# Convolution chain on one core: products of layer 0 ordered by row groups, waves of the tail joined into two double waves a step

## The chip, the core and the metric

The kernel runs on one core of one Trainium2 chip. The metric is the device time of one execution in microseconds (us). The kernel before takes 5648.19 us, the median of three runs (5645.71 to 5648.49). Differences below about 0.2%, some 11 us, can't be told from no change here.

## What is computed

The input x is 4 x 16 x 512 x 512 in f32 (batch, channels, rows, columns). Four layers follow each other. Cut to what matters:

```python
# layer 0: depthwise 3x3 convolution added to x, attention in 8x8 windows (2 heads of 8), MLP
x = x + depthwise3x3(x, pos_w) + pos_b
q, k, v = qkv(aff1(x))                      # per window of 64 positions
x = x + softmax(q @ k.T * 8**-0.5) @ v @ proj_w.T + proj_b
x = x + gelu(aff2(x) @ fc1_w.T + fc1_b) @ fc2_w.T + fc2_b
# layer 1: fake-quantised 3x3 convolution, batch norm over the whole output, clip to 0..6
z = clip(batch_norm(conv3x3(quant(x), quant(weight))), 0, 6)
# layer 2: two 3x3 convolutions with a residual
x = conv3x3(relu(conv3x3(z, w1) + b1), w2) + b2 + z
# layer 3: 3x3 convolution, then 16 -> 128 -> 16 pointwise, with a residual
out = x + w2 @ relu(w1 @ conv3x3(x) + b1) + b2
```

## The kernel before

**Three stretches.** The layer 0 stretch (`window_attention`, L144) lasts to about 3150 us; a statistics pass of layer 1 (L1026 to L1053) has its products from 3166 to 3449 us; and the tail, with its first product at 3461 us, runs layers 1 to 3 as one pipeline over 128 groups of rows (L1228 to L1242) to the end. In all of them the order of instructions on each engine is the order in which the code emits them (`manual_schedule`): every engine works its list in order and waits where an operand or a buffer isn't ready.

**Layer 0.** There are 64 steps. A step has 128 partitions (four row quarters of 32, called quads) and four column parts of 512 positions. The helper `quad(i)` picks partitions 32i to 32i+31. Most products are 32x32 weights against 512 positions: the input's quad selects a row group of the TensorE array, the output's quad a column group. Such an f32 product appears in the trace as two records of its line, so 16 products of all 16 tiles are 32 records.

A step first runs the score part (`values`, `scores`, `attend`, `divide`, `turn_back`, L519 to L541). Then come 16 blocks "qqddddqqqqdddddd" (L543): a "q" is a query product of the next step (L314, evicted by ACT at L319 here), a "d" is one tap of the depthwise convolution of the step after (L287), four products of one row group. The queries use PSUM banks 4, 5, 6, 7, 4, 5 in this order (L542). Then `project(y)` (L547, products at L404) multiplies the attention output `o` by the two heads' weights, 2 x 16 products, into the same banks 4 to 7: part u goes into bank 4 + (u + 2) % 4, that is 6, 7, 4, 5. DVE adds each bank to `y[:, u]` (L409, four instructions, u = 0 first). After that 44 blocks "ddddhdhddhqq..." (L558) run; an "h" is the hidden layer of the MLP for one part (L416, evicted by ACT with GELU at L421) and reads `y[:, u]`, the first three with u = 0.

Ahead of the loop, the depthwise convolution of steps 0 and 1 runs alone: nine taps of 16 products each (L489 to L492), row group u outside, column part vv inside.

**The tail.** Step T runs these on TensorE, in this order: `outputs(T-7)` (L1217, 16 products of 128x32 weights), `wave(T-6, 0)` (L1197, four products of 32x128 weights, one a row group), `stage_y(T-4)`, `wave(T-6, 1)`, `stage_x(T-3)`, `wave(T-6, 2)`, `stage_h(T-1)`, `stage_z(T)`, `wave(T-6, 3)`. The four stages are 3x3 convolutions of 24 products of 64x32 weights each (`convolve`, L1122; `stage_z` in bf16). PSUM banks are handed out in rotation by `take` (L961): 2 for a convolution, 4 for a wave, 2 for the outputs, of 8 in all. A convolution's first bank is evicted by ACT and its second by DVE (L1181/L1182 for `stage_y`, L1159/L1160 for `stage_h`, L1141/L1142 for `stage_z`); both banks of `stage_x` by DVE (L1170). The banks of a wave are evicted by DVE (L1207, first and third) and ACT (L1205, second and fourth). DVE also scales the next input (L1010), clips `ze` in place (L1143) and adds the outputs (L1223).

SP issues the DMAs of a step in the order of the code: the load of T+3 (L940, 2), the store of the outputs (L1226, 1), and four each for `qo` (after the rounding on ACT, L1013), `xo`, `ho` and `zo` (L1064 and L1067), which copy a stage's rows to the partitions where the next stage reads them.

Of the kernel before, what the change touches and what calls it, by code (L numbers as in the profile page):

```python
# [29 lines left out]
TP = H // 4  # L30
NH, HD = 2, 8
WS = 8
T = WS * WS
# [71 lines left out]
def conv_chain(ctx: ExitStack, tc: tile.TileContext, x, xw, mats, vecs, cqs, cws, hots, out):  # L105
# [29 lines left out]
    nc.gpsimd.memset(peak, 0.0)  # L135

    safe = window_attention(tc, xw, x1, hots, m, v, peak)
    with tc.If(safe == 0):
        attention_block(tc, x, x1, m, v, peak)
# [4 lines left out]
def window_attention(ctx: ExitStack, tc, xw, x1, hots, m, v, peak):  # L144
# [15 lines left out]
    U = V = 4  # L160
# [14 lines left out]
    def bank(i):  # L175
        return pairs[i // 2][:, i % 2, :] if i < 4 else singles[i - 4]

    def quad(i):
        return slice(32 * i, 32 * i + 32)
# [3 lines left out]
    def load(k):  # L183
        t = xin.tile([P, V, WS + 2, BW + 2], F32, tag="x", name=f"x{k}")
        nc.sync.dma_start(t, xw[k])
        return t
# [93 lines left out]
    def by_row(ap):  # L280
        return ap.rearrange("p (a j x) -> p a j x", a=WS, x=WS)

    def depthwise(n, tap, u):

        dy, dx = divmod(tap, 3)
        for vv in range(V):
            nc.tensor.matmul(  # L287
                bank(u)[quad(vv)], taps[quad(u), tap, :],
                xts[n][quad(u), vv, dy : dy + WS, dx : dx + BW],
                start=tap == 0, stop=tap == 8,  # L290
            )

    def position(n, i):

        if n not in ys:
            ys[n] = px.tile([P, U, N], F32, tag="y", name=f"y{n}", bufs=3)
        for u in (2 * i, 2 * i + 1):
            nc.vector.tensor_scalar(  # L298
                by_window(ys[n][:, u]), by_row(bank(u)), v("pos_b"), None, ALU.add
            )  # L300
# [98 lines left out]

    def project(y):  # L400
        for h in range(NH):
            for u in range(U):
                for vv in range(V):
                    nc.tensor.matmul(  # L404
                        bank(4 + (u + 2) % 4)[quad(vv)], wo[h][quad(u)], o[quad(u), vv, :, h, :],
                        start=h == 0, stop=h == 1,
                    )
        for u in range(U):
            nc.vector.scalar_tensor_tensor(  # L409
                y[:, u], bank(4 + (u + 2) % 4), pb, y[:, u], ALU.add, ALU.add  # L410
            )
# [76 lines left out]
    )  # L488
    for n in range(2):  # L489
        for tap in range(9):  # L490
            for u in range(U):
                depthwise(n, tap, u)  # L492
        xts[n + 2] = load(n + 2)
        for i in range(2):
            position(n, i)
# [8 lines left out]
    for n in range(STEPS):  # L504
# [40 lines left out]
        if more:  # L545
            highest(n + 1)
        y = ys.pop(n)  # L547
        project(y)
        if n % 2 == 0:
            xo = px.tile([P, U, WS, XW], F32, tag="xo", name=f"xo{n}", bufs=1)  # L550
# [5 lines left out]
        hids, units, sent = [[] for _ in range(U)], itertools.cycle((6, 7, 4, 5)), 0  # L556
        used = [0] * U
        for i, what in enumerate("ddddhdhddhqqhddhdhddhdhddhddhddhdhddddhhddhh"):  # L558
            if what == "h":
                at = i % 4  # L560
                u = used[at]
# [364 lines left out]
def _quad(i):  # L926
    return slice(32 * i, 32 * i + 32)
# [19 lines left out]
def conv_layers(ctx: ExitStack, tc, x1, out, cw, cq, sw, m, v, peak):  # L947
# [13 lines left out]
    def take(n):  # L961
        return [banks[next(turn) % 8] for _ in range(n)]
# [3 lines left out]
    def ring(name, n, dt=F32):  # L966
        tiles = rings[name] = [
            act.tile([P, 2, WP], dt, name=f"{name}{i}") for i in range(n)
        ]
        return lambda k: tiles[k % n]  # L970
# [6 lines left out]
    ze, zo, he, ho = ring("ze", 4), ring("zo", 3), ring("he", 2), ring("ho", 2)  # L977
# [19 lines left out]
    def inner(t):  # L997
        return t[:, :, 1 : W + 1]
# [3 lines left out]
    def load(n, dst=None):  # L1002
        if dst is None:
            dst = ld.tile([P, 2, W], F32, tag="x", name=f"tx{n}")
        loaded[n] = dst
        _load_pairs(nc, dst, x1, n)
# [62 lines left out]
    def quantised(n):  # L1069
        scaled(n)  # L1070
        rounded(n)
        shift(n, qe, qo, n < TP)
# [39 lines left out]
    def convolve(weights, pair):  # L1112

        p = take(2)
        for dx in range(3):
            for w in range(2):
                if pair[w] is None:
                    continue
                src, odd = pair[w]
                for f in range(2):  # L1120
                    for r in range(2):
                        nc.tensor.matmul(  # L1122
                            p[r][_quad(2 * f + w)], weights[_half(r), odd, dx, :],
                            src[_half(r), f, dx : dx + W],
                            start=dx == 0, stop=dx == 2,
                        )
        return p

    def shift_ends(n, e, o):

        shift(n, e, o, ends=True)
        if n == TP - 1:
            for i in (0, 2):
                nc.gpsimd.memset(o(n)[_quad(i)], 0.0)

    def stage_z(n):

        if not 0 <= n < TP:
            return
        p, z = convolve(cq, ((qe(n), 0), (qo(n), 1))), inner(ze(n))  # L1140
        nc.scalar.activation(z[:, 0], p[0], AF.Identity, bias=shift_by, scale=scale)  # L1141
        nc.vector.tensor_scalar(z[:, 1], p[1], scale, shift_by, ALU.mult, ALU.add)  # L1142
        nc.vector.tensor_scalar(z, z, ACT_MAX, 0.0, ALU.min, ALU.max)  # L1143
        shift_ends(n, ze, zo)

    def stage_h(n):

        if not 0 <= n <= TP:
            return
        second = (ze(n), 0) if n < TP else None  # L1150
        p, h = convolve(cw[:, 0], ((zo(n - 1), 1), second)), inner(he(n))
        if n in (0, TP):
            e = slice(n // TP, n // TP + 1)
            for f in range(2):
                nc.scalar.activation(
                    h[:, f], p[f], AF.Relu, bias=edge_b1[:, e], scale=v("edge")[:, e]
                )
        else:
            nc.scalar.activation(h[:, 0], p[0], AF.Relu, bias=v("l2_b1"))  # L1159
            nc.vector.tensor_scalar(h[:, 1], p[1], v("l2_b1"), 0.0, ALU.add, ALU.max)  # L1160
        shift(n, he, ho, n < TP)

    def stage_x(n):

        if not 0 <= n < TP:
            return
        p = convolve(cw[:, 1], ((he(n), 0), (ho(n), 1)))
        x, z = inner(xe(n)), inner(ze(n))
        for r in range(2):
            nc.vector.scalar_tensor_tensor(  # L1170
                x[:, r], p[r], v("l2_b2"), z[:, r], ALU.add, ALU.add
            )
        shift_ends(n, xe, xo)

    def stage_y(n):

        if not 0 <= n <= TP:
            return
        second = (xe(n), 0) if n < TP else None
        p, y = convolve(cw[:, 2], ((xo(n - 1), 1), second)), inner(ye(n))  # L1180
        nc.scalar.copy(y[:, 0], p[0])  # L1181
        nc.vector.tensor_copy(y[:, 1], p[1])  # L1182
# [5 lines left out]
    def wave(n, k):  # L1188

        if not 0 <= n < TP:  # L1190
            return []
        units, p = [], take(4)
        for q in range(4):
            w, f = divmod((k + q) % 4, 2)
            par = w ^ (q % 2)
            src = ye(n + (w and not q % 2))
            nc.tensor.matmul(  # L1197
                p[q], w1[_quad(q), 1 - par, :], inner(src)[_quad(q), f, :],
                start=True, stop=True,
            )  # L1200
        for q in range(4):
            w, f = divmod((k + q) % 4, 2)
            hd = ld.tile([P, W], F32, tag="hid", name=f"hid{n}_{k}_{q}", bufs=24)
            if next(count) % 2:
                nc.scalar.activation(hd, p[q], AF.Relu, bias=v("l3_b1"))  # L1205
            else:
                nc.vector.tensor_scalar(hd, p[q], v("l3_b1"), 0.0, ALU.add, ALU.max)  # L1207
            units.append((q // 2, 2 * f + w, w ^ (q % 2), hd))
        return units

    def outputs(n, units):

        if not units:
            return
        p, o, seen = take(2), inner(xe(n)), set()
        for r, c, par, hd in units:
            nc.tensor.matmul(  # L1217
                p[r][_quad(c)], w2[:, par], hd,
                start=(r, c) not in seen, stop=(r, c) in seen,
            )  # L1220
            seen.add((r, c))
        for r in range(2):
            nc.vector.scalar_tensor_tensor(  # L1223
                o[:, r], p[r], v("l3_b2"), o[:, r], ALU.add, ALU.add
            )
        nc.sync.dma_start(out[n], o)  # L1226

    units = []  # L1228
    for T in range(TP + 7):
        if T + 3 <= TP:  # L1230
            load(T + 3)
        outputs(T - 7, units)
        units = wave(T - 6, 0)
        stage_y(T - 4)
        units += wave(T - 6, 1)
        if T + 2 <= TP:
            quantised(T + 2)
        stage_x(T - 3)
        units += wave(T - 6, 2)
        stage_h(T - 1)  # L1240
        stage_z(T)
        units += wave(T - 6, 3)  # L1242


def _strips(a):
# [127 lines left out]
```

## Time and profile before

| What | us |
|---|---|
| median of three runs | 5648.19 |
| profiled execution, its own time | 5653.74 |
| its span, first to last instruction | 5651.9 |
| PE busy | 5441.0 (96%) |
| DVE busy | 3826.3 (68%) |
| ACT busy | 3427.9 (61%) |
| POOL busy | 707.4 (13%) |
| products of `project`, L404, in 64 steps | 105.1 to 3123.7 |
| products of the waves, L1197 | 3527.0 to 5641.4 |

The page lists busy time by engine. PE's busy time counts a product from its start to its modelled end, so 96% says that nearly always some product is under way, not that the array is full: 16 small tiles or one may be at work. What matters is where products start late. A record's line in the timeline gives its start, the time from the first start to the last end of merged records, the engine, the line, the operation, output and inputs, how many records were merged (x8), and in brackets the idle time of that engine before it and what ended it.

### The profile page before, as it was taken

How to read it: one execution, taken by the hardware profiler on the slowest of the kernel's cores; microseconds unless marked ns; L12 is line 12 of the kernel's file. 1: busy time of each engine (PE TensorE's matmuls, PEld its weight loads, DVE VectorE, ACT ScalarE, POOL GpSimd, SP SyncE). 2: the span in 40 equal slices, each digit the busy share in tenths (PEclk: the TensorE clock that was granted, in tenths of full speed). 3: DMA queues.
4: the chain of work that ended last, by engine and by line, in shares of the span. 5: the costliest groups of instructions: out<-in, count | busy, mean ns of one | idle time of the engine just before them, and what ended most of it. 6: DMA issues, size and time to landing. Idle time of an engine off the chain costs nothing. (4 is left out here: it accounts for less than half of the span.)

```text
span 5651.9 us, 268227 instructions
## 1 busy us (share of the span) xinstructions
PE 5441.0 (96%) x120912; PEld 2960.7 (52%) x120912; DVE 3826.3 (68%) x5934; ACT 3427.9 (61%) x4610; POOL 707.4 (13%) x692
## 2 busy tenths in 40 slices
PE   7999999999999999999999666999999999999999
PEld 5777777767677777777776332222222222222222
DVE  4667666666667766666666454667677676777676
ACT  3777777777777777777777453444444444444444
POOL 1111111111111111111111452000000000000000
PEclk9999999999999999999999898999999999999999
DMA  2333333332333333333332797767777767777774
GB/s 79 78 76 77 77 74 80 73 80 66 77 72 82 73 82 73 80 73 80 74 79 41 167 246 178 174 174 178 173 178 173 177 173 176 175 175 175 175 177 107
DMA packets 626192, 677.45 MB, mean 120 GB/s; under 512 B 355856, under 2 KB 485008, under 8 KB 616848
## 3 DMA queue, kind: packets, MB, share of 16 engines
q1 hardware_dynamic: 624240, 658.76, 48.6%
q8 instruction: 953, 15.61, 1.2%
q14 instruction: 199, 1.63, 0.1%
q0 software_dynamic: 512, 1.05, 0.1%
q10 hardware_dynamic: 288, 0.39, 0.0%
HBM read 222.45 MB, written 134.48 MB: 63 GB/s over the span
## 5 line engine op out<-in xcount | busy, mean ns | idle before, releaser
L356 ACT ACTIVATE e<-pair 128x1024 f32<-128x1024 f32 x1024 | 993.0, 1022 | 488.8 <-PE pair L348 488.1
L287 PE MATMUL pair<-x,taps 32*32 32x512 f32 x18432 | 1043.2, 603 | 4.2 <-issue 2.4
L1205 ACT ACTIVATE hid<-tb,vec 128x512 f32<-128x512 f32 x1024 | 647.8, 685 | 630.4 <-PE tb L1197 630.4
L384 DVE STREAM_TRANSPOSE a<-bank 128x512 f32<-128x512 f32 x1024 | 669.7, 692 | 320.2 <-PE bank L369 298.6
L391 POOL TENSOR_TENSOR t<-a,r 128x512 f32<-128x512 f32 x512 | 542.0, 1059 | 2561.3 <-DVE r L389 2561.3
L421 ACT ACTIVATE hid<-bank,f1b 128x512 f32<-128x512 f32 x1024 | 653.5, 687 | 332.7 <-PE bank L416 245.7
L348 PE MATMUL pair<-g,y 32*128 32x128 f32 x16384 | 757.7, 286 | 3.7 <-issue 2.0
L1207 DVE TENSOR_SCALAR hid<-tb,vec 128x512 f32<-128x512 f32 x1024 | 718.2, 744 | 27.1 <-PE tb L1197 26.8
L348 PEld LDWEIGHTS pair<-g,y 32*128 32x128 f32 x16384 | 650.5, 186 | 153.5 <-issue 136.6
L416 PE MATMUL bank<-y,fc_e 32*32 32x512 f32 x8192 | 722.3, 610 | 0.6 <-DVE y L409 0.4
L369 PE MATMUL bank<-e,yt 64*32 64x128 f32 x32768 | 604.1, 274 | 22.4 <-ACT e L356 12.8
L287 PEld LDWEIGHTS pair<-x,taps 32*32 32x32 f32 x18432 | 531.3, 103 | 164.6 <-issue 54.8
L1197 PE MATMUL tb<-ye,mat 32*128 32x512 f32 x4096 | 586.1, 639 | 0.0
L369 PEld LDWEIGHTS bank<-e,yt 64*32 64x32 f32 x32768 | 459.6, 106 | 122.1 <-issue 92.1
L1217 PE MATMUL tb<-hid,mat 128*32 128x512 f32 x4096 | 466.0, 595 | 0.0
L298 DVE TENSOR_SCALAR y<-pair,vec 128x512 f32<-128x512 f32 x256 | 180.3, 747 | 349.8 <-PE pair L287 349.8
L1122 PE MATMUL tb<-zo,cw 64*32 64x512 f32 x3096 | 365.7, 598 | 16.2 <-issue 8.9
L1122 PE MATMUL tb<-xo,cw 64*32 64x512 f32 x3096 | 360.5, 592 | 5.9 <-ACT hid L1205 2.1
L1122 PE MATMUL tb<-ho,cw 64*32 64x512 f32 x3072 | 358.4, 592 | 3.7 <-issue 3.2
L1197 PEld LDWEIGHTS tb<-ye,mat 32*128 32x128 f32 x4096 | 162.8, 183 | 377.5 <-issue 370.4
L1122 PE MATMUL tb<-ze,cw 64*32 64x512 f32 x3072 | 359.9, 598 | 0.0
L1122 PE MATMUL tb<-he,cw 64*32 64x512 f32 x3072 | 358.1, 592 | 0.0
(178 smaller groups left out, 7111.1 us busy)
## 6 DMA issues: line engine op xcount, KB each, us to landing
x<-in_xw_dram SPq DMA_DIRECT2D x64, 1320.0 KB, 5.7
zo<-ze SPq DMA_DIRECT2D x512, 128.5 KB, 2.4
ho<-he SPq DMA_DIRECT2D x512, 128.5 KB, 2.4
xo<-xe SPq DMA_DIRECT2D x512, 128.5 KB, 2.4
y<-y SPq DMA_DIRECT2D x2048, 32.0 KB, 2.7
tx<-x SPq DMA_DIRECT2D x256, 256.0 KB, 4.0
out_dram<-xe SPq DMA_DIRECT2D x128, 512.0 KB, 4.6
x<-xo SPq DMA_DIRECT2D x1008, 64.0 KB, 2.8
```

Source lines behind the costliest of these rows:

```text
L287: nc.tensor.matmul(bank(u)[quad(vv)], taps[quad(u), tap, :], xts[n][quad(u), vv, dy : dy + WS, dx : dx + BW], start=tap == 0, stop=tap == 8,)
L348: nc.tensor.matmul(bank(u)[:, P * jj : P * jj + P], y2[quad(u), vv, jl + jj].rearrange("p w t -> p (w t)"), g[quad(u), vv, jl + jj].rearra ...
L356: nc.scalar.activation(e[:, 2 * i : 2 * i + 2].rearrange("p u j t -> p u (j t)"), pairs[i], AF.Exp,)
L369: nc.tensor.matmul(bank(4 + 2 * (k % 2) + w)[quad(u), P * jj : P * jj + P], t[half, U * jj + u, w : w + 2].rearrange("p d c -> p (d c)"), ...
L384: nc.vector.transpose(a[:, 512 * w : 512 * w + 512], bank(4 + 2 * (k % 2) + w))
L391: engine.tensor_tensor(t.rearrange("p b w c -> p w b c"), top, r.unsqueeze(3).to_broadcast([P, 2, 16, C]), ALU.mult,)
L416: nc.tensor.matmul(b[quad(k)], fc1[quad(vv), quad(k)], y[quad(vv), u, :], start=True, stop=True,)
L421: nc.scalar.activation(hd, b, AF.Gelu, bias=f1b)
L1122: nc.tensor.matmul(p[r][_quad(2 * f + w)], weights[_half(r), odd, dx, :], src[_half(r), f, dx : dx + W], start=dx == 0, stop=dx == 2,)
L1197: nc.tensor.matmul(p[q], w1[_quad(q), 1 - par, :], inner(src)[_quad(q), f, :], start=True, stop=True,)
L1205: nc.scalar.activation(hd, p[q], AF.Relu, bias=v("l3_b1"))
L1207: nc.vector.tensor_scalar(hd, p[q], v("l3_b1"), 0.0, ALU.add, ALU.max)
```

## The change

In layer 0, `project` loops over the column part vv outside and over the row group u inside, where it was the other way round; so the first four products go into four banks. The lone depthwise taps of steps 0 and 1 get the same order. The blocks "d" in the loop stay as they were.

In the tail, the waves are emitted in pairs. The order on TensorE in step T is now `stage_y(T-4)`, waves 0 and 1 of T-6, `stage_x(T-3)`, `stage_h(T-1)`, `stage_z(T)`, waves 2 and 3 of T-6, `outputs(T-6)`. The outputs follow their waves in the same step and no longer open the next one. The clip of `ze` and the `zo` DMAs leave `stage_z` for a function of their own, which runs behind waves 2 and 3; so on DVE the clip stands behind the evictions of these waves, and on SP the order is load, qo, xo, ho, zo, store. The loop has one step less.

```diff
-    def depthwise(n, tap, u):
+    def depthwise(n, tap, u, strips=range(V)):
 
         dy, dx = divmod(tap, 3)
-        for vv in range(V):
+        for vv in strips:
...
     def project(y):
         for h in range(NH):
-            for u in range(U):
-                for vv in range(V):
+            for vv in range(V):
+                for u in range(U):
...
         for tap in range(9):
-            for u in range(U):
-                depthwise(n, tap, u)
+            for vv in range(V):
+                for u in range(U):
+                    depthwise(n, tap, u, (vv,))
...
         nc.vector.tensor_scalar(z[:, 1], p[1], scale, shift_by, ALU.mult, ALU.add)
+
+    def capped(n):
+
+        if not 0 <= n < TP:
+            return
+        z = inner(ze(n))
         nc.vector.tensor_scalar(z, z, ACT_MAX, 0.0, ALU.min, ALU.max)
         shift_ends(n, ze, zo)
...
-    units = []
-    for T in range(TP + 7):
+    for T in range(TP + 6):
         if T + 3 <= TP:
             load(T + 3)
-        outputs(T - 7, units)
-        units = wave(T - 6, 0)
         stage_y(T - 4)
-        units += wave(T - 6, 1)
+        units = wave(T - 6, 0) + wave(T - 6, 1)
         if T + 2 <= TP:
             quantised(T + 2)
         stage_x(T - 3)
-        units += wave(T - 6, 2)
         stage_h(T - 1)
         stage_z(T)
-        units += wave(T - 6, 3)
+        units += wave(T - 6, 2) + wave(T - 6, 3)
+        capped(T)
+        outputs(T - 6, units)
```

## The prediction, made before the changed kernel was run

> **What bounds the kernel now.** I read the page's busy times first (PE 5441.0 of 5651.9 us), then the waits on other engines, then the timeline at the edges of the instructions that the change moves. In the tail one step lasts 16.715 us (from the first `xo` product of one step to that of the next, constant within 0.01 us over some 120 steps), and PE is never without work there. So what counts is how closely its products follow each other.
>
> ```profile
> 4602.34 0.61 PE L1122 MATMUL tb<-xo,cw 64*32 64x512 f32 x4
> 4602.36 0.61 PE L1122 MATMUL tb<-xe,cw 64*32 64x512 f32 x4
> 4602.76 0.61 PE L1122 MATMUL tb<-xo,cw 64*32 64x512 f32 x4
> 4602.79 0.61 PE L1122 MATMUL tb<-xe,cw 64*32 64x512 f32 x4
> 4603.33 1.14 PE L1197 MATMUL tb<-ye,mat 32*128 32x512 f32 x8
> 4603.49 0.59 ACT L1181 COPY ye<-tb 128x512 f32<-128x512 f32 x1 [1.44 <-PE tb L1122]
> 4603.60 0.69 DVE L1182 COPY ye<-tb 128x512 f32<-128x512 f32 x1 [1.20 <-PE tb L1122]
> ...
> 4604.40 0.63 PE L1122 MATMUL tb<-he,cw 64*32 64x512 f32 x4
> ```
>
> Inside a convolution a new pass of eight records starts every 0.429 us. A wave is two passes, yet 1.07 us go by from its start (4603.33) to the next convolution's (4604.40), and 0.565 instead of 0.429 us from the last pass (4602.763) to it. Also to be seen: when a wave starts, the convolution before it has just begun to be evicted. ACT is done at 4604.08, DVE at 4604.29.
>
> The same at the end of the bf16 stage, where DVE still has an eviction in front:
>
> ```profile
> 4611.20 0.75 DVE L1160 TENSOR_SCALAR he<-tb,vec 128x512 f32<-128x512 f32 x1 [1.18 <-issue]
> ...
> 4611.59 1.14 PE L1197 MATMUL tb<-ye,mat 32*128 32x512 f32 x8
> 4611.70 0.78 ACT L1141 ACTIVATE ze<-tb,shift,scale 128x512 f32<-128x512 f32 x1
> 4611.87 0.80 DVE L1142 TENSOR_SCALAR ze<-tb,scale,shift 128x512 f32<-128x512 f32 x1
> ```
>
> In layer 0 I looked at `project` and who releases it:
>
> ```profile
> 1393.80 2.43 ACT L319 ACTIVATE g<-bank,gb 128x512 f32<-128x512 f32 x4 [1.08 <-PE bank L314]
> ...
> 1394.96 0.68 PE L404 MATMUL bank<-o,wo 32*32 32x512 f32 x4
> ...
> 1396.28 0.66 PEld L404 LDWEIGHTS bank<-o,wo 32*32 32x32 f32 x33 [0.43 <-ACT g L319]
> ...
> 1397.53 2.73 DVE L409 SCALAR_TENSOR_TENSOR y<-bank,pb,y 128x512 f32<-128x512 f32 x4 [1.13 <-issue]
> ...
> 1398.49 0.66 PE L416 MATMUL bank<-y,fc_e 32*32 32x512 f32 x4
> ```
>
> ACT evicts the last query (bank 5) at 1396.23, 1.27 us after `project` began; the weight load released by it comes 0.05 us later. In the 21 steps that I counted, never more than 24 records, that is 12 products, have started by then: exactly those ahead of part u = 3, whose bank is 5. So PE doesn't go past a waiting product. The first hidden product (L416) follows DVE's first L409.
>
> **What the Trainium skill says.** "TensorEngine Tiling (Array Packing)", Key Properties: a change of tiling mode drains the array. The trace agrees: convolution to wave costs 0.136 us beyond the 0.429, wave to convolution 0.108, wave to outputs 0.109; convolution to bf16 convolution (same tiles) nothing. "TensorE: Matmul & The Clock Gate", LDWEIGHTS: a load takes its columns / 1.2 ns, 107 ns for 128 and 27 ns for 32. That fits what is exposed after a drain: a wave's first pass lasts 0.534 instead of 0.429 us, a convolution's 0.454. The same page, Part 3, The mechanism: loads overlap running products only in another row group. In the lone taps, four products of one row group in succession, 32 records take 1.074 us at full clock, where 2 x 0.429 = 0.858 would do; in the convolutions, which alternate row halves, 0.429 holds.
>
> **The tail, cost by cost.** Of a step's 16.715 us, 15.229 are passes (three f32 convolutions 3 x 6 x 0.429, bf16 0.643, four waves 8 x 0.429, outputs 8 x 0.429); 1.486 are eight changes of mode with their exposed loads. Left over are five: convolution to double wave twice (0.136 + 0.105 each), double wave to convolution (0.108 + 0.025), to outputs (0.109 + 0.024), and outputs to convolution. The last isn't in the trace; it lies between 0.108 and 0.138, and I take 0.12 + 0.025. Sum 0.895: 0.59 us a step is saved.
>
> Two waits are new. `take` hands eight banks to a double wave, all there are, and the last two are those of the convolution just finished. Second wave of the first pair: its third product needs ACT's copy (done at 4604.08), its fourth DVE's copy, done at 4604.29. From DVE's end to a released weight load 0.085 us go by (L409 to L416), and the load of 128 columns is then exposed (0.105), so it streams from 4604.48 instead of 4604.31: 0.18 us. Second wave of the second pair: DVE is done at 4611.87 + 0.80 = 4612.67; streaming from 4612.86 instead of 4612.575 gives 0.29. PE stands in these waits with the rest of the step queued behind it. Bounds: nothing, if the evictions came in time (the trace says no), or 0.07 + 0.18 if only the product waits and its load doesn't; I take 0.47. What remains is 0.12 us a step, 128 x 0.12 = 15 us saved (bounds 0 and 76).
>
> What is merely moved: DVE evicts four banks of a double wave (4 x 0.67) before it scales the next input, which comes 1.36 us later in the step; rounding and the 16 copies on SP (about 0.6 us each, in before from 7.2 to 18.4 us after the step's start) shift with it. The last `xo` copy is issued at 12.47 + 1.36 = 13.8 and lands 2.4 later, at 16.2; the next `stage_y` wants it at 16.6. Cover 0.4 us, and beyond that each late us costs one. The clip comes behind eight evictions; its reader, the `stage_h` of the next step, is some 9 us away, and `zo` lands in 2.4. Store behind `zo`, load behind the store: their waits end about 1.5 us into the next step, the queue needs SP next at 8.5, and a load has a whole step of slack. All this I cost at nothing. The outputs read hidden tiles that DVE finishes 2 us before their turn. The missing last loop step saves nothing: its one member moved up.
>
> **Layer 0, cost by cost.** Product 4 of `project` now needs bank 5, where product 13 did. Its wait ends 1.02 us (mean of 62 steps) after `project`'s start, 1.27 in the latest. The nine products that ran under it now come after it. From then each array tile still has up to four records, at 0.429 each: the bank of u = 0 is complete 0.05 + 3 x 0.429 + 0.07 + 0.59 = 2.0 us after the eviction; DVE begins 0.1 later, takes 0.75, the hidden product comes 0.09 later: 2.94. In before it comes 2.33 after it (mean), since u = 0 was finished first. Per step, with the later of the eviction and 0.3 us after the start, I get 0.61 us in the mean (0.17 to 0.68). PE reaches the hidden block after four taps at about 2.7 and then sits. Nothing takes it up again: from the first hidden product to the next step's first transpose there are 11.29 to 11.51 us in every step. 63 steps with queries x 0.61 = 38 us lost. Bounds: a gain of 0.43 a step (the rate alone, 2.15 to 1.72 us) and a loss of 0.9, if the new order isn't packed better. The DVE waits on `o` move from product 3 to 9 and 13; `turn_back` is done by 0.09 us, so nothing. The lone taps: about twelve at full clock x 0.215 = 2.6 us saved; at half clock passes already follow at 0.854.
>
> **Sum.** +38 - 2.6 - 15 = +20 us: 5674 against the profiled execution's 5653.74. That one lies 5.5 above the median, so 5668 against the median of 5648.19.
>
> **Rivals.**
> - *Faster: the double waves run through.* If evictions release the last products in time or the array works ahead, the tail saves all of 0.59 x 128 = 76 us: 5648 + 38 - 3 - 76 = 5608. For it: PE alone has no slack in the tail. Against: the DVE ends above. It decides where the pair's stalls fall below 0.2 us together, since then 50 us saved outweigh layer 0.
> - *`project` costs nothing.* If PE's reordering hides the bank wait, or the first hidden product comes no later, 5648 - 3 - 15 = 5630; with the full rate gain 5603. Against it: the count of 24.
> - *The `xo` copy becomes the bound.* If it lands 0.3 us late in every step, the tail loses 0.2 instead of gaining: 5648 + 35 + 23 = 5706. For it: only 0.4 us of cover; against: the order on SP is unchanged there.
>
> **Chances.** Main case 0.56, with its own range 5655 to 5685; double waves free or nearly so 0.17; `project` free 0.15; `xo` bound 0.12. Within 0.2% (11 us, about what a measurement can tell from no change) fall the edges of the first three: 0.17. Faster 0.23, slower 0.60. The range 5615 to 5696 leaves out the far halves of the rivals, about 0.2.
>
> **What would show it.** Tail period 16.6 (16.1 for the first rival, over 16.7 for the third); in the fourth product of the second and fourth wave a wait on DVE. In `project`, the fourth product released by L319, L409 starting 2.1 us after it, a step longer by 0.6 (47.8 now). I am wrong if the hidden product doesn't move, or if the wave pairs show eight records every 0.429 us through both waves.

## The result, and the profile after

The changed kernel takes 5684.09 us (median of six runs, 5661.89 to 5695.48), the kernel before 5644.1 us (six runs, the three from above among them, 5614.89 to 5648.49). The ratio is 1.0066 with a 95% interval of 1.0045 to 1.0087: about 37 us slower by the ratio, 40 by the medians. The forecast was 5668 us, slower, with a range of 5615 to 5696.

The profiled execution took 5688.79 us. Its span and the page's busy times:

```profile
span 5687.0 us, 268595 instructions
...
PE 5479.1 (96%) x120912; PEld 3103.8 (55%) x120912; DVE 3825.7 (67%) x5934; ACT 3409.7 (60%) x4610; POOL 708.7 (12%) x692
```

The number of instructions on PE is the same as before, and so is its share of 96%. Its busy time has grown by 38 us, the span by 35: products that stand less densely appear as more busy time and not as idle time. The page's first part doesn't tell where the time went. Three stretches do, cut at records that every kernel of this study has: the first and the last product of `project` (in the kernel before its start at 3124.5 us; the 3123.7 above is that of its weight load), and the tail's first product on `xo`, which is the start of the pipeline's fourth stage (3503.8 us in the kernel before) and not the first product of all at 3461 us. "The tail" in the tables is what follows it, up to the end:

| us | first to last product of `project` | from there to the first `xo` product | tail | end |
|---|---|---|---|---|
| before | 3019.4 | 379.3 | 2148.1 | 5651.9 |
| after | 3065.6 | 373.4 | 2140.8 | 5687.0 |
| the stretch unchanged, in all kernels of this study | 3019.4 to 3025.7, mean 3022.2 (7) | 360.1 to 379.3 (13) | 2148.1 to 2153.5, mean 2151.2 (8) | |

The number of kernels stands in parentheses. The middle stretch differs by 19 us from execution to execution, and nearly all of this falls before the tail begins: from the last product of `project` to the first one after the statistics pass (L1081 in the kernel before) go 315.8 to 334.8 us, with the same code in all but `project_more_taps`, which isn't at an edge of that range. So it is scatter and not an effect of an edit. The outer two repeat within some 6 us, so an edit is priced by its own stretch. Against the means of the last row, layer 0 has lost 43 us and the tail has won about 10.5.

**Layer 0.** The timeline of the kernel after at one `project`; columns as in the prediction's fences.

```profile
1229.22 2.42 ACT L319 ACTIVATE g<-bank,gb 128x512 f32<-128x512 f32 x4 [1.45 <-PE bank L314]
...
1230.83 2.73 PE L404 MATMUL bank<-o,wo 32*32 32x512 f32 x49
...
1231.69 0.60 PEld L404 LDWEIGHTS bank<-o,wo 32*32 32x32 f32 x33 [0.45 <-ACT g L319]
...
1234.04 1.41 DVE L409 SCALAR_TENSOR_TENSOR y<-bank,pb,y 128x512 f32<-128x512 f32 x2 [2.08 <-issue]
1234.84 0.13 PEld L416 LDWEIGHTS bank<-y,fc_e 32*32 32x32 f32 x5 [0.62 <-DVE y L409]
```

ACT's fourth eviction ends at 1231.64, and the weight loads that it releases come 0.05 us later. DVE's first add (L409) starts 2.40 us after that eviction's end, and the hidden product's load is now released by DVE, with 0.62 us of idle time of the loads ahead of it. In the kernel after the first hidden product's load waits for DVE in all 64 steps, in the kernel before in 4 of them.

**The tail.** The timeline of the kernel after around both double waves of one step.

```profile
4609.34 0.61 PE L1123 MATMUL tb<-xe,cw 64*32 64x512 f32 x4
...
4609.88 2.14 PE L1204 MATMUL tb<-ye,mat 32*128 32x512 f32 x16
4610.04 0.59 ACT L1188 COPY ye<-tb 128x512 f32<-128x512 f32 x1 [4.99 <-PE tb L1123]
...
4610.15 0.69 DVE L1189 COPY ye<-tb 128x512 f32<-128x512 f32 x1 [1.45 <-PE tb L1123]
...
4611.95 0.63 PE L1123 MATMUL tb<-he,cw 64*32 64x512 f32 x4
...
4617.94 2.23 PE L1204 MATMUL tb<-ye,mat 32*128 32x512 f32 x16
...
4618.19 0.80 DVE L1143 TENSOR_SCALAR ze<-tb,scale,shift 128x512 f32<-128x512 f32 x1
...
4620.10 0.64 PE L1224 MATMUL tb<-hid,mat 128*32 128x512 f32 x4
```

Sixteen records of L1204 now stand together, where two groups of eight stood. From a double wave's start to the next stage 2.07 us (4609.88 to 4611.95) and 2.16 us (4617.94 to 4620.10) go by. Four passes of 0.429, the load exposed at the start (0.105) and the change of mode (0.108) would make 1.93; so 0.14 and 0.23 are lost. The single records show where: in both double waves the fourth product of the second half starts 0.055 us after the end of DVE's eviction (0.054 or 0.055 in 203 of the 205 between 3800 and 5500 us), while its three neighbours are ahead of it. The period of the tail is 16.525 us in the common step and 16.596 us in the mean of the full steps, against 16.715.

### The profile page after: what moved, and what is told of

It reads as the page before. It is cut to its first block, busy times and chain, and to the rows that moved or that the text cites. A ratio compares the mean times of both kernels' runs of the same rounds, so it can differ in the third digit from the quotient of the medians.

```text
span 5687.0 us, 268595 instructions
## 1 busy us (share of the span) xinstructions
PE 5479.1 (96%) x120912; PEld 3103.8 (55%) x120912; DVE 3825.7 (67%) x5934; ACT 3409.7 (60%) x4610; POOL 708.7 (12%) x692
## 5 line engine op out<-in xcount | busy, mean ns | idle before, releaser
L287 PE MATMUL pair<-x,taps 32*32 32x512 f32 x18432 | 1092.4, 602 | 3.3 <-DVE y L298 1.7
L416 PE MATMUL bank<-y,fc_e 32*32 32x512 f32 x8192 | 724.0, 599 | 1.6 <-DVE y L409 1.4
L1214 DVE TENSOR_SCALAR hid<-tb,vec 128x512 f32<-128x512 f32 x1024 | 697.6, 744 | 39.7 <-PE tb L1204 27.1
L1212 ACT ACTIVATE hid<-tb,vec 128x512 f32<-128x512 f32 x1024 | 620.4, 689 | 111.8 <-PE tb L1204 111.5
L287 PEld LDWEIGHTS pair<-x,taps 32*32 32x32 f32 x18432 | 519.9, 103 | 168.2 <-issue 59.1
L1204 PE MATMUL tb<-ye,mat 32*128 32x512 f32 x4096 | 564.2, 622 | 0.0
L1188 ACT COPY ye<-tb 128x512 f32<-128x512 f32 x129 | 75.8, 587 | 662.0 <-PE tb L1123 662.0
L1204 PEld LDWEIGHTS tb<-ye,mat 32*128 32x128 f32 x4096 | 255.7, 183 | 261.6 <-issue 219.6
L1123 PE MATMUL tb<-xo,cw 64*32 64x512 f32 x3096 | 372.6, 601 | 9.3 <-issue 7.5
L1123 PE MATMUL tb<-xe,cw 64*32 64x512 f32 x3072 | 361.9, 601 | 0.0
```

Source lines behind the costliest of these rows:

```text
L287: nc.tensor.matmul(bank(u)[quad(vv)], taps[quad(u), tap, :], xts[n][quad(u), vv, dy : dy + WS, dx : dx + BW], start=tap == 0, stop=tap == 8,)
L416: nc.tensor.matmul(b[quad(k)], fc1[quad(vv), quad(k)], y[quad(vv), u, :], start=True, stop=True,)
L1123: nc.tensor.matmul(p[r][_quad(2 * f + w)], weights[_half(r), odd, dx, :], src[_half(r), f, dx : dx + W], start=dx == 0, stop=dx == 2,)
L1204: nc.tensor.matmul(p[q], w1[_quad(q), 1 - par, :], inner(src)[_quad(q), f, :], start=True, stop=True,)
```

## The experiments

All start from the kernel before and make the edit that is named. H is the time from the first record of `project` to the first hidden product (L416), mean of 61 steps; "last query eviction" is ACT's eviction of bank 5 at the edge of `project`.

### Each part alone

`tail_only` has the changed tail, with layer 0 as before. `project_only` and `taps_only` are the kernel before with one loop order each:

```diff
 # project_only
-            for u in range(U):
-                for vv in range(V):
+            for vv in range(V):
+                for u in range(U):
```

> The change in the tail alone, layer 0 as before. If the tail gained what its period says (16.716 to 16.596 us), the time falls by about 15 us against the kernel before, and the whole loss of the changed kernel, some 55 us, belongs to layer 0. If the tail gains more and layer 0 loses less than its steps say (rival: part of the lost time is clock and start-up noise), it falls by 0 or by over 30 us.

> The new order of project alone. Theory (bank wait, and u = 0 complete last): the first hidden product comes 4.23 us after project's start instead of 3.34, 62 x 0.89 = 55 us slower. Rival (the new order only exposes another start-up or clock state): within 10 us of the kernel before.

> The new order of the lone taps of steps 0 and 1 alone. As predicted (loads of other row groups overlap): 32 records in 0.86 us at full clock, 2.6 us faster. As the changed kernel's trace suggests: 1.074 us in both orders, no change, within 3 us.

| | median us | ratio to before, 95% interval | own stretch, against its unchanged mean |
|---|---|---|---|
| `tail_only` | 5638.61 | 0.999 [0.9973, 1.0008] | tail 2140.5, -10.7 |
| `project_only` | 5701.96 | 1.0103 [1.0074, 1.0131] | layer 0 3069.4, +47 |
| `taps_only` | 5653.55 | 1.001 [0.9999, 1.0021] | first product of `project` at 107.9; 105.1 to 107.1 in the kernels with the old taps |

So the loss is the loop order of `project`, as `project_only` by itself shows. The tail is a small gain, too small for the timing, but plain in the stretch: no unchanged tail is shorter than 2148.1. The taps give nothing. Each kernel with one part has the value of the kernel after for that part (4.23 and 16.596) and that of the kernel before for the other (`project_only`: H 4.21, period of the tail 16.715; `tail_only`: H 3.34, 16.611), so the parts add up without acting on each other.

### Which half of `project`

Two effects of the new order could delay the first add. With head 0 by rows, product 4 already waits for bank 5, and little is started before. With head 1 by rows, the bank of u = 0 is finished only with the last products. Two kernels have one effect each.

```diff
 # rows_head1; rows_head0 has (rows_first, parts_first)
+        parts_first = [(u, vv) for u in range(U) for vv in range(V)]
+        rows_first = [(u, vv) for vv in range(V) for u in range(U)]
         for h in range(NH):
-            for u in range(U):
-                for vv in range(V):
+            for u, vv in (parts_first, rows_first)[h]:
```

> Of project, head 0 in the order of before (bank 5 first needed by product 13), head 1 by row groups first (u = 0 complete at product 29 of 32). If the wait for bank 5 is the whole loss, no change. If the late completion of u = 0 has a part of its own, the first L409 starts some 1.9 us after the eviction of bank 5 instead of 1.45, 25 to 35 us slower.

> Of project, head 0 by row groups first (bank 5 needed by product 4), head 1 in the order of before (u = 0 complete at product 20). The counterpart alone, head 1 by row groups first, cost 0.70 of the 0.89 us a step. If the two parts add up, this one costs the rest, 0.19 us a step, 12 us. If both share one cost (29 products are queued behind bank 5 either way, and a tile's four records in a chain set when u = 0 is complete), it costs 0.5 to 0.6 us a step, some 35 us.

The timeline of `rows_head1`, where ACT's last query eviction ends at 1221.65:

```profile
1219.23 2.42 ACT L319 ACTIVATE g<-bank,gb 128x512 f32<-128x512 f32 x4 [1.19 <-PE bank L314]
...
1220.84 2.58 PE L405 MATMUL bank<-o,wo 32*32 32x512 f32 x50
...
1223.85 2.07 DVE L410 SCALAR_TENSOR_TENSOR y<-bank,pb,y 128x512 f32<-128x512 f32 x3 [1.84 <-issue]
```

The timeline of `rows_head0`, where it ends at 1221.61:

```profile
1219.19 2.42 ACT L319 ACTIVATE g<-bank,gb 128x512 f32<-128x512 f32 x4 [0.93 <-PE bank L314]
...
1223.73 2.07 DVE L410 SCALAR_TENSOR_TENSOR y<-bank,pb,y 128x512 f32<-128x512 f32 x3 [1.32 <-issue]
```

Means over the steps (the start of the first add and of the last record are counted from the end of the last query eviction):

| | records of `project` started before that end, at most | last record | first add | H | layer 0 stretch | ratio |
|---|---|---|---|---|---|---|
| before | 24 | 1.64 | 1.45 | 3.34 | 3019.4 | |
| `rows_head1` | 24 | 1.64 | 2.22 | 4.04 | 3060.1 | 1.0086 [1.0056, 1.0116] |
| `rows_head0` | 6 | 1.78 | 2.13 | 3.94 | 3052.0 | 1.0052 [1.0032, 1.0071] |
| `project_only` | 6 | 1.78 | 2.41 | 4.21 | 3069.4 | 1.0103 [1.0074, 1.0131] |
| after | 6 | 1.77 | 2.40 | 4.23 | 3065.6 | 1.0066 [1.0045, 1.0087] |

Each half alone costs most of the whole: 0.70 and 0.60 us in H, 0.87 to 0.89 together. They overlap and don't add. In `rows_head1` the wait for the bank is as before and the last record starts no later, yet the first add comes 0.77 us later: a record lasts 0.59, and the add starts about where the last record of all ends (1.64 + 0.59 = 2.23). This is more than the 1.9 that was expected. In the kernel before the add starts ahead of that end (1.45), since the bank of u = 0 is finished before the others. In `rows_head0` that lead is there, but the start of the products is held up. In the kernel after, the early start and the lead are both gone: 1.77 + 0.59 = 2.36, and the add starts at 2.40.

### One part after the other

If a bank finished early is what counts, then u outside and the heads inside should finish it earliest.

```diff
-        for h in range(NH):
-            for u in range(U):
+        for u in range(U):
+            for h in range(NH):
```

> Project with u outermost, then head, then column part: bank 5 is needed by product 25 of 32 and u = 0 is complete after 8. If the first L409 is what matters, it starts as soon as DVE has its long reduce behind it (about 2.25 us after project's start, 2.47 in before), and a step gains up to 0.2 us, at most 12 us in all; if PE's own work up to the first hidden product is the bound there (some 3.2 us), at most 5 us, which a run can't tell from none. A loss would speak against the theory.

Result 5695.87 us, ratio 1.0077 [1.0058, 1.0096]; layer 0 stretch 3066.8, +45. The gain that I expected is a loss. The timeline of this kernel, with the end of the last query eviction at 1226.77:

```profile
1224.34 2.43 ACT L319 ACTIVATE g<-bank,gb 128x512 f32<-128x512 f32 x4 [1.21 <-PE bank L314]
...
1227.57 2.76 DVE L409 SCALAR_TENSOR_TENSOR y<-bank,pb,y 128x512 f32<-128x512 f32 x4 [0.39 <-issue]
1228.84 0.64 PE L404 MATMUL bank<-o,wo 32*32 32x512 f32 x4
1229.54 0.66 PE L416 MATMUL bank<-y,fc_e 32*32 32x512 f32 x4
```

DVE does begin early, 0.80 us after the eviction here and 1.24 in the mean. But PE itself is late: it still starts records of `project` at 1228.84, in the mean until 2.56 us after the eviction against 1.64 before, and the hidden products stand behind them (H 4.21). Of the 48 records ahead of part u = 3, only 15.6 in the mean had started when the eviction ended, while in the kernel before 18.5 of the 24 ahead of it had. So an early first bank isn't enough. What sets this order apart is that eight products of one row group follow each other, where there were four; that this is the price fits, but wasn't tried apart.

### More work ahead of the first hidden product

If PE merely sits while it waits for the add, work put there should cost nothing. On `project_only`, four more taps go ahead of the first "h":

```diff
-"ddddhdhddhqqhddhdhddhdhddhddhddhdhddddhhddhh"
+"ddddddddhhqqhdhhdhddhdhddhddhddhdhddddhhddhh"
```

> The new order of project alone, with eight taps instead of four ahead of the first hidden product (two hidden products trade places with later taps). If PE stands idle for y[:, 0] in the new order, the taps fill that time, and from project's start to the next step's first transpose some 0.3 us or more a step come back (15.70 us with the new order, 14.77 before). If PE is itself late there, nothing comes back.

Result 5716.74 us, ratio 1.0104 [1.0078, 1.013]; layer 0 stretch 3092.9. A "d" is eight records here, so four are 32 records, 1.07 us of work by the lone taps. H rose by only 0.32 (4.53), so by this estimate about 0.75 us of it went into time that was unused before. But the time from the first hidden product to the next step's first transpose didn't fall (11.51 against 11.49), though this work was taken out of it. The waits of 1000 us of layer 0 (1000 to 2000) tell why; columns: total us, times, longest. `project_only`:

```profile
PEld bank L416 <- DVE y L409: 21.0, 40, 0.6
...
PEld bank L416 <- ACT hid L421: 7.4, 20, 0.4
```

`project_more_taps`:

```profile
PEld bank L416 <- ACT hid L421: 20.3, 40, 0.6
```

The wait for DVE (3.5 us in the kernel before) has left this place, and the hidden products, now closer together, wait for ACT's evictions instead. The run shows that the first hidden product can be covered; its time doesn't show what the loss is made of, since the order that covers it meets ACT. The records tell a part: in the kernel after no product at all starts in the last 0.30 us before the first hidden one (mean; 0.05 in the kernel before, 0.27 in `rows_head1`, 0.05 in `rows_head0`). So some 0.25 of the 0.89 us is a pause of PE, and the rest is products that start later or less densely.

### The tail: which wait costs, and who is behind

Three kernels on top of `tail_only` shift what stands around the second double wave.

```diff
 # tail_quant
-        if T + 2 <= TP:
-            quantised(T + 2)
         stage_x(T - 3)
+        if T + 2 <= TP:
+            quantised(T + 2)
```

```diff
 # tail_swap
-        stage_h(T - 1)
         stage_z(T)
+        stage_h(T - 1)
```

> The change in the tail alone, with the quantising step behind stage_x, so that on SP the xo copies go ahead of the qo copies. If the 25 longer steps (up to 17.45 us) come from xo landing late, all steps last 16.53 us and it is 9 us faster than the tail change alone. If they come from something else, they stay.

> The change in the tail alone, with stage_z ahead of stage_h, so that no eviction is queued on DVE ahead of the last one that the second double wave waits for. If the queue on DVE makes the difference between the two waits (0.25 against 0.15 us), that wait falls to 0.15 and the common step to 16.42 us, 12 us faster than the tail change alone. If the wait is set otherwise, the step stays at 16.53.

| | period, common step | period, mean | steps over 0.1 us late (of some 120) | tail | ratio |
|---|---|---|---|---|---|
| before | 16.715 | 16.715 | 0 | 2148.1 | |
| after | 16.525 | 16.596 | 23 to 25 | 2140.8 | |
| `tail_quant` | 16.967 | 16.983 | 3 | 2188.7 | 1.0059 [1.004, 1.0078] |
| `tail_swap` | 16.455 | 16.524 | 21 | 2132.0 | 0.9973 [0.9964, 0.9982] |

In the kernel after (and in `tail_only`) every fifth step or so is longer, by up to 0.9 us. The waits of the tail in the kernel after (3700 to 5600) have a row that the kernel before doesn't have:

```profile
PEld tb L1123 <- DMA xo<-xe: 10.6, 15, 0.8
```

The `xo` copies land too late there. `tail_quant` moves scaling, rounding and the `qo` copies behind `stage_x`, so that the `xo` copies are earlier on SP. The late steps all but vanish, as expected; but its timeline shows a greater price:

```profile
4618.74 1.15 ACT L1013 ACTIVATE qe<-tx,unround 128x1024 bf16<-128x1024 f32 x1 [3.47 <-DVE tx L1010]
4619.76 2.55 PE L1203 MATMUL tb<-ye,mat 32*128 32x512 f32 x16
...
4620.36 0.77 ACT L1141 ACTIVATE ze<-tb,shift,scale 128x512 f32<-128x512 f32 x1
...
4622.24 0.64 PE L1223 MATMUL tb<-hid,mat 128*32 128x512 f32 x4
```

The expectation was a gain of 9 us against `tail_only`. But the rounding (1.15 us) is in front of the two evictions on ACT, the eviction of `ze` starts 0.60 us into the double wave, and this takes 2.49 us instead of 2.16. That is the wait which the prediction priced, made longer: the double wave pays for an eviction that isn't done when its second half starts.

`tail_swap` is the opposite: with the bf16 stage in front, the stage just ahead of the second double wave is the longer `stage_h`, so that no eviction is queued on DVE ahead of the one that counts. Its timeline:

```profile
4619.51 2.15 PE L1203 MATMUL tb<-ye,mat 32*128 32x512 f32 x16
4619.63 0.69 ACT L1165 ACTIVATE he<-tb,vec 128x512 f32<-128x512 f32 x1 [1.77 <-PE tb L1122]
4619.73 0.75 DVE L1166 TENSOR_SCALAR he<-tb,vec 128x512 f32<-128x512 f32 x1 [1.20 <-issue]
...
4621.59 1.06 PE L1223 MATMUL tb<-hid,mat 128*32 128x512 f32 x8
```

Both evictions have begun within 0.22 us of the double wave's start, which takes 2.08 us here (median 2.089). The common step is 0.07 us shorter. But the queue isn't the main reason: DVE's eviction ends 0.984 us after the double wave's start, against 1.057 in `tail_only`, and of these 0.07 us the earlier start makes only 0.02 (0.234 against 0.255). The other 0.05 is that the eviction of `he` is shorter than that of `ze` (0.751 against 0.802; medians of some 100 steps). The fourth product follows its end by 0.055 us here too. This kernel, with layer 0 as before, takes 5632.95 us and is faster than the kernel before and the changed one. Late steps remain (21).

`tail_sent_last` tries to remove those too: on `tail_swap`, only the `qo` copies go behind `stage_x`; scaling and rounding (`quantised` with False) stay.

```diff
-            quantised(T + 2)
+            quantised(T + 2, False)
         stage_x(T - 3)
+        if T + 2 <= TP:
+            shift(T + 2, qe, qo, T + 2 < TP)
         stage_z(T)
```

> The change in the tail alone, with stage_z ahead of stage_h, and with the qo copies issued on SP behind the xo copies, while scaling and rounding stay where they are. If the late steps come from the xo copies standing behind the qo copies, they vanish and every step lasts 16.45 us, 9 us faster than with the stages swapped alone; about 30 us below the kernel before. If they have another cause, some 20 of 120 steps stay long.

Result 5640.3 us, ratio 0.9974 [0.9965, 0.9984], no better than `tail_swap`. The late steps have gone (4 left, and no row for `xo` among the waits), but the common step is 16.541 instead of 16.455: `stage_h` takes 2.855 us instead of 2.740. The timeline of its first products:

```profile
4618.44 0.63 PE L1123 MATMUL tb<-he,cw 64*32 64x512 f32 x4
4618.48 0.75 PE L1123 MATMUL tb<-ho,cw 64*32 64x512 f32 x4
```

Four records of `he` are done within 0.63 us, four of `ho` beside them take 0.75: some tiles lag by 0.12 to 0.15, pass after pass, until the array changes its mode. In the records this lag starts in `stage_x` of this order: the second `ho` product there waits for two DMA semaphores and starts 0.125 us after its neighbour, where in `tail_swap` each of these products waits for one. That the second semaphore is the cause was read from the trace and not tried by itself.

### The lone taps

The prediction put their rate (1.074 us for 32 records, 0.858 at the full rate) down to weight loads within one row group. `taps_pairs` keeps four products of one row group in succession, but uses two row groups at a time, 8 of the 16 tiles:

```diff
-        for tap in range(9):
-            for u in range(U):
-                depthwise(n, tap, u)
+        for i in range(2):
+            for tap in range(9):
+                for u in (2 * i, 2 * i + 1):
+                    depthwise(n, tap, u)
```

> The lone taps over two row groups at a time, all nine taps, then the other two; four products of one row group still in succession. If loads within a row group stretch the passes, a pass of the eight tiles still takes over 0.5 us at full clock. If it is the number of products that PE can look ahead over, 16 being too many, a pass takes 0.429 us with eight. In either case this part of the kernel is slower, since half the array is used.

Single execution, 5666.76 us, beside a median of 5652.09 before; first product of `project` at 117.9 us instead of 105.1. The timeline of the lone taps in the kernel after:

```profile
36.40 4.15 PE L287 MATMUL pair<-x,taps 32*32 32x512 f32 x117
```

and in `taps_pairs`:

```profile
53.41 4.13 PE L287 MATMUL pair<-x,taps 32*32 32x512 f32 x69
```

In `taps_pairs` passes of eight records start at 54.205, 54.635, 55.064 and 55.493: every 0.429 us, the full rate, with four products of one row group in succession. In the kernel after, with row groups alternating, taps start at 37.364, 38.437 and 39.511, again 1.07 us for 32 records. So neither the row group nor the order sets that rate; in these runs it appears only with all 16 tiles in use. With half of the tiles the same work takes longer as a whole.

## Why the prediction was right, and where it was off

The direction, the place of the loss and the signs of the two large stretches came as written. Sum by stretches: layer 0 +45 (the mean of this kernel's 43 and the 47 of `project_only`; forecast +38), tail -10.5 (forecast -15), taps 0 (forecast -2.6). That is +35, against +20 forecast and 37 timed: all three terms were too favourable to the change, and the time came out near the edge of the main case's own range (5655 to 5685).

- **`project`: the mechanism held, its size was off.** Product 4 is released by L319, at most 6 records start before, and the hidden product waits for L409. The step that was too small is "at 0.429 each: the bank of u = 0 is complete 0.05 + 3 x 0.429 + 0.07 + 0.59 = 2.0 us after the eviction": it puts the last record's start at 1.41, and measured were 1.77, nearly a pass more. So L409 starts 2.40 and not 2.1 after the eviction, and the hidden product moves by 0.88 and not by 0.61. I took four passes at full rate although the lone taps, whose rate the prediction itself gives, show that with 16 tiles it isn't reached: with their 0.537 a pass (1.074 / 2) the last start would have been put at 1.73.
- **The cause within it was only half named.** The prediction ties the late bank of u = 0 to the wait for bank 5. The two half orders show that the late finish of u = 0 costs as much with that wait left as it was (0.70 in H, against 0.60 for the wait moved alone).
- **"Nothing takes it up again"** held in the MLP part (11.42 to 11.49 us, even 0.07 longer). But the mean period of layer 0 grew by 0.72 us (47.97 to 48.69, the stretch over its 63 periods, the unchanged kernels against the two with the edit), less than 0.88 + 0.07: the score part that follows is about 0.2 shorter. The reason wasn't looked into.
- **The tail's stalls** were priced at 0.18 and 0.29, measured 0.14 and 0.23. The fourth product of the second double wave lags by up to 0.25 us behind its neighbours and starts 0.055 after DVE's `ze` eviction ends: the mechanism is the predicted one. Mis-sized in part was "From DVE's end to a released weight load 0.085 us go by": 0.085 is the time to the hidden product in a kernel in which that seldom waits for DVE. Where a load of L416 does wait for L409, 40 times in the kernel before, it comes 0.051 to 0.053 us after its end. The change from outputs to convolution, never seen before, costs 0.113 beyond a pass (the prediction took 0.12). "TensorEngine Tiling (Array Packing)", Key Properties, that a change of mode drains the array, agrees with this too. (The load records themselves last 0.104 us for 32 columns, L404, and 0.184 for 128, L1197. So the columns / 1.2 ns of the prediction fit what is exposed and the 0.08 between the two records, but each record is 0.08 longer than the rule has it.) The common step gains 0.19 us, more than the 0.12 forecast.
- **What I costed at nothing took part of it back.** The cover of 0.4 us of the `xo` copies fails in every fifth step: 0.07 us a step in the mean, and 0.12 remain. It is the third rival in small. That the 0.12 is the forecast's own figure is luck: a gain that was too small by 0.07 met a loss of 0.07 that was put at nothing. And the end of the tail isn't free: from the last `xo` stage to the end go 26.2 instead of 24.9 us, and the four steps ahead of it take 0.7 us more. I had multiplied by 128 and let the ends cost nothing. The first three steps take 49.0 us, which isn't shown to be an effect: 43.7 to 49.1 in the unchanged tails, 46.8 in the mean. Of 0.12 x 121 full steps = 14.5 us, 10.5 remain against the mean of the unchanged tails; against the profiled execution of before, whose start is the shortest of all, only 7.
- **The taps: the reason fell.** The forecast gain rested on "TensorE: Matmul & The Clock Gate", Part 3, The mechanism, that loads overlap only in another row group; the section names a second way, a background weight buffer, which the prediction left out. In `taps_pairs` loads inside one row group don't slow the passes at all, and alternating row groups don't speed them up with 16 tiles. The measurement decides.
- **The rivals.** Double waves that run through fall by the 2.07 and 2.16 us. A free `project` falls by `project_only`. `xo` as the bound in every step falls by the common step of 16.525.

**Open.** What stretches passes when 16 tiles are in use isn't settled: a limit to how many products PE looks ahead would fit the records (those of the next tap start late, in a bunch), but no run tells it from others. The pause of PE ahead of the first hidden product is 0.25 of the 0.89 us lost at `project`; what the rest is made of isn't separated. Nor is it known why PE falls behind in `u_outermost`.

## What to carry to other kernels

Ask which operand or bank the next engine wants first, and order products so that it is complete first; an order that fills all banks evenly finishes all of them last. Then ask which bank comes free last, and put its products last. Neither rule is enough: `u_outermost` obeys both and loses 45 us, since the engine that fills the banks falls behind itself. So count the records that have started at a fixed moment, before and after. Joining small groups saves changes of mode, but a joined group that takes every bank waits for the eviction just begun, so put ahead of it the stage whose eviction ends soonest. A queue shifted by more than its cover shows up in some steps only: look at the spread of the period, not only at its common value, and price the ends of a pipeline apart.

## What the hardware showed that I had not expected

- Four f32 products of one row group in succession run at a pass per 0.429 us with 8 tiles in use, while 32 records over 16 tiles take 1.07 us in either order.
- Records of some tiles that fall 0.12 to 0.15 us behind in one product stay behind, through three convolutions, until the next change of mode (`tail_sent_last`).
- In both double waves, with either stage ahead, the product that needs the last bank starts 0.054 to 0.055 us after the end of DVE's eviction of it (the medians in four kernels).
- The same code between layer 0 and the tail took 315.8 to 334.8 us in 12 executions of 12 kernels, a greater spread than the whole gain of the tail; a stretch cut at fixed records is a better scale for an edit than the whole time.
